# Maximum over keys and inverse of the weight sums carried to all partitions by VectorE transpositions and transfers instead of products; weights loaded once per image

## The chip, the cores and the metric

The kernel runs on one core of one Trainium2 chip. A core has five engines that run side by side, each with its own queue of instructions worked off in order: TensorE (PE, matrix products), VectorE (DVE), ScalarE (ACT), GpSimd (POOL) and SyncE (SP, which only issues transfers here). They wait for each other by semaphores. Products go from SBUF into PSUM; transfers (DMA) move data between SBUF and DRAM and are issued from the queues of SP, ACT and POOL. The metric is the device time of one execution in microseconds, as the median of several runs.

## The reference

Four images of 256 channels and 64x64 pixels go through two layers. The first is self-attention over the N = 4096 pixels with heads of 32 channels for query and key and 256 for the value:

```python
q = jnp.einsum('oc,bcn->bno', wq, xf) + bq
k = jnp.einsum('oc,bcn->bon', wk, xf) + bk[None, :, None]
attn = jax.nn.softmax(jnp.einsum('bnd,bdm->bnm', q, k), axis=-1)
v = jnp.einsum('oc,bcn->bon', wv, xf) + bv[None, :, None]
out = jnp.einsum('bcn,bmn->bcm', v, attn).reshape(B, Cc, H, W)
return gamma[0] * out + x
```

The second layer is a group norm, a clustering step (projections `f_w`, `v_w`, cosine similarity to four centres, sigmoid, one-hot of the largest, aggregation, projection back), a second group norm with an MLP of 1024 hidden channels and gelu, two batch norms with relu and a last 256x256 product. All is float32.

## The kernel before

The attention keeps keys on partitions and queries on the free axis. The 4096 queries are 8 blocks of 512 (`NB`), and for each block the 4096 keys are 8 groups of four tiles of 128. One block with one key group is a *unit*; an image has 64 units, numbered u = 8·nb + g.

- `score(u)` computes 4 products with 32 contraction rows (line 333) into two PSUM tiles. ScalarE copies them to an SBUF slot (lines 351 and 356), and VectorE keeps the running maximum over keys in `top` (lines 353 to 358): for each of the 128 partitions and each query, over all tiles so far.
- `fold(nb)` halves `top`; then `across(nb)` has TensorE transpose it in four pieces (line 369), VectorE reduce each (line 371) and lay the maxima on diagonals (`dg`, line 373); `spread` has TensorE multiply a matrix of ones with them (line 383), which puts the maximum of each query onto every partition of `mb` in PSUM. This must be done once for each block before its exponentials.
- `exps(u)`: VectorE subtracts `mb` in place (line 395), ScalarE takes the exponential (line 398), POOL adds the weights to `acc` (lines 400 and 403).
- `weigh(u, av, quarter)`: TensorE multiplies the weights with the value tile into two PSUM accumulators `av` (line 408), 8 instructions for each unit, each in two passes.
- After the block: `gather` (POOL, line 420) adds both halves of `acc`; `total` (line 429) multiplies with ones, so that the sum over all partitions stands on every partition; ScalarE copies it out (line 430), `inverse` takes the reciprocal in four pieces (line 435), `add` on POOL scales and adds the residual (lines 439 and 444).

The order is written out by hand: `weighting` runs over the 64 units and for each calls `exps(u + 1)`, the score that is due `LEAD` = 9 units ahead, the four quarters of `weigh`, and the pieces for the block before (`total` at g = 0, `inverse` at 1 and 2, `add` at 3, statistics at 5). `across` for the next block stands in unit g = 6, `spread` in g = 7. Scores live in `SLOTS` = 10 buffers of the pool `spool`, which also holds the image tiles. In images 1 to 3 the scores of the first block have been computed in the MLP of the image before; units 0 to 5 then catch up with one score every three quarters. Block 0 of each image has its maximum spread outside the loop (`alone`, or `maximum` and `first`).

After the 64 units come the cluster stage (it writes the normalised centres into the margins of `mix`, the weights for `f` and `v`, lines 115 and 703) and the MLP with `w1_s` and `w2_s`. These, and `mix`, are loaded once at the start; `derived`, called in unit 1 of image 0, turns two quarters of `w1_s` into a sum and a negative (lines 185 and 186), as the MLP uses them. SP's queue carries the loads of x (line 81) and the output (line 1115). The last block of each image already takes its sums in four products of 32 output rows (line 578).

Of the kernel before, what the change touches and what calls it, by code (L numbers as in the profile page):

```python
# [28 lines left out]
RG, GRP = 4, N // NB  # L29
LEAD, SLOTS = 9, 10  # L30

# [14 lines left out]
def attention_then_cluster_block(  # L46
# [22 lines left out]

    spool = ctx.enter_context(tc.tile_pool(name="spool", bufs=N // XT + SLOTS))  # L70
    work = ctx.enter_context(tc.tile_pool(name="work", bufs=2))
# [3 lines left out]
    ps_m = ctx.enter_context(tc.tile_pool(name="ps_m", bufs=2, space=PSUM))  # L75

    def load_x(b, t):
# [34 lines left out]

    wfv_l = spool.tile([P, KC, 2 * ED], F32, tag="s", name="wfv_l")
    nc.sync.dma_start(out=wfv_l, in_=wfv.rearrange("(k p) m -> p k m", p=P))
    mix = const.tile([P, KC, 2, 2 * ED + 32], F32, name="mix")
    for f in range(2):
        nc.gpsimd.tensor_copy(mix[:, :, f, 16 : 16 + 2 * ED], wfv_l)
    fvb = const.tile([P, 2 * ED], F32, name="fvb")
# [5 lines left out]
    nc.sync.dma_start(out=wproj_s[ED:, :], in_=pc[:, ipb : ipb + 1].rearrange("c o -> o c"))  # L124
    w1_s = loaded("w1_s", w1.rearrange("(k p) m -> p k m", p=P), [P, KC, HID])
    w2_s = loaded("w2_s", w2.rearrange("(k p) m -> p k m", p=P), [P, HID // P, C])
    wpw_s = loaded("wpw_s", wpw.rearrange("(k p) m -> p k m", p=P), [P, KC, C])
# [35 lines left out]
    ab = const.tile([P, 2], F32, name="ab")  # L163
    fb_w = const.tile([ED, P], F32, name="fb_w")
    wf_t = const.tile([ED, C], F32, name="wf_t")

    W_A, W_CD = w1_s[:, 0, : HID // 2], w1_s[:, 0, HID // 2 :]
    W_B, W_D = w1_s[:, 1, : HID // 2], w1_s[:, 1, HID // 2 :]

    def derived():  # L170
# [13 lines left out]

        nc.gpsimd.tensor_tensor(W_CD, W_CD, W_D, ALU.add)
        nc.gpsimd.tensor_scalar(W_D, W_D, -1.0, None, ALU.mult)

        nc.vector.tensor_scalar(gbv, gbv, pvc("gamma"), None, ALU.mult)
# [4 lines left out]
        for k in range(KC):  # L193
            nc.tensor.transpose(
                tps[:ED, k * P : (k + 1) * P], mix[:, k, 0, 16 : 16 + ED], ident
            )
# [49 lines left out]
    def attention(b, xs):  # L246
# [118 lines left out]
        def across(nb, tag="w2"):  # L365
# [13 lines left out]
            return dg  # L379

        def spread(nb, dg):
            mxs[nb] = ps_m.tile([P, NB], F32, tag="m", name=f"mb_{b}_{nb}")
            nc.tensor.matmul(  # L383
                mxs[nb], ones, dg.rearrange("p j n -> p (j n)"), start=True, stop=True
            )
# [40 lines left out]

        def total(nb):
            den = ps_m.tile([P, NB], F32, tag="m", name=f"den_{b}_{nb}")
            nc.tensor.matmul(den, ones, rdens[nb], start=True, stop=True)  # L429
# [33 lines left out]
        def alone():  # L463

            nc.vector.tensor_scalar(fb_w, ones[:ED], pvc("f_b", ED), None, ALU.mult)
            k_half(0)
# [44 lines left out]
        def weighting(ahead, fill, early):  # L511
            dg, av = None, None

            biased = {u: (i // KC, i % KC) for i, u in enumerate((3, 4, 5, 6, 20, 28, 36, 44))}
            for u in range(units):
# [106 lines left out]
    def cluster(b, ys, stats, cells, rest, fill, gelu):  # L622
# [9 lines left out]
        ga, gb = group_norm(b, "gn1", stats, fill, pooling)  # L632
        xns = {}

# [322 lines left out]
    def late_block(b, y, gab):  # L957
# [24 lines left out]
        def first(j, k):  # L982
            if k == 0:
# [5 lines left out]
                held["p"],  # L989
                w1_s[:, k, j * P : (j + 1) * P],  # L990
                x[:, 1, 0] if k and j >= 4 else x[:, 0, k],
# [10 lines left out]
        def second(j, c):  # L1002
            if j == 0:
                held["a", c] = ps_m.tile([P, NB], F32, tag="m", name=f"mol_{b}_{c}")
            nc.tensor.matmul(
                held["a", c],
                w2_s[:, j, c * P : (c + 1) * P],
                hidden(j),
# [42 lines left out]
    def mlp(b, ys, stats2, fill, nxt, blocks):  # L1051

        w_bcd, w_bac, w_abcd = (
# [320 lines left out]
```

## Time and profile before

| What | Time |
|---|---|
| median of 3 runs | 3479.46 us (3477.38 to 3481.62) |
| the profiled execution | 3478.09 us |
| its span | 3476.0 us |
| TensorE busy | 3421.1 us, 98% |
| VectorE busy | 2046.2 us, 59% |
| ScalarE busy | 1683.9 us, 48% |
| POOL busy | 1489.2 us, 43% |
| granted TensorE clock | 0.997 |
| `tt`, transposition (line 369), one pass | 273 ns, x128 |
| `mb`, spreading product (line 383), one pass | 592 ns (median), x64 |
| `den`, sum (line 429), one pass | 592 ns, x56 |

A product in float32 appears as two passes in the trace, each with its weight load (PEld); a transposition appears as one. Passes overlap, so the time that one takes from the queue is the distance between starts and not its duration. A row of the profile names the line, the engine, the operation, output and inputs, the shape, and how often; in a timeline the start and the time of the merged run stand in front, and the bracket at the end tells how long the engine had been idle and for whom. Lines of the waits give the total in microseconds, the number, and the longest.

### The profile page before, as it was taken

The numbers are of one execution on the slowest core, as the hardware profiler recorded it, in microseconds if no ns is written. First come the engines' busy times: TensorE is split into PE (matmuls) and PEld (weight loads), VectorE is DVE, ScalarE is ACT, GpSimd is POOL, SyncE is SP. The second block draws the span as 40 slices with busy tenths as digits, with TensorE's granted clock in tenths as the row PEclk, the third lists the DMA queues.
The fourth block names the chain that finished last, engine by engine and source line by source line (L and its number), as shares of the span: only waits on it lengthen the run. The fifth ranks groups of instructions, "written<-read, shape, count | busy, mean of one in ns | idle before, by whom it ended". The sixth has DMA issues, their size and how long they took to land.

```text
span 3476.0 us, 31760 instructions
## 1 busy us (share of the span) xinstructions
PE 3421.1 (98%) x11760; PEld 1694.3 (49%) x11760; DVE 2046.2 (59%) x2912; ACT 1683.9 (48%) x2157; POOL 1489.2 (43%) x799
## 2 busy tenths in 40 slices
PE   8999999999999999999999999999999999999999
PEld 4444445655444444565544444466554444445565
DVE  4666664645566666464556666646446666664543
ACT  5545553444554554344455555434445554544444
POOL 2656665211265665521126566552104665672200
PEclk9999999999999999999999999999999999999999
DMA  2000001000000000100000000000000000000000
GB/s 91 7 4 3 7 0 49 7 19 13 20 5 4 3 7 12 37 7 19 19 16 4 3 5 5 19 30 7 19 19 10 4 7 3 4 0 1 13 19 25
DMA packets 25260, 47.16 MB, mean 14 GB/s; under 512 B 6704, under 2 KB 8592, under 8 KB 25104
## 3 DMA queue, kind: packets, MB, share of 16 engines
q1 hardware_dynamic: 20240, 38.29, 3.2%
q10 hardware_dynamic: 4608, 6.30, 0.8%
q8 instruction: 93, 1.52, 0.2%
q0 software_dynamic: 256, 0.52, 0.1%
q14 instruction: 63, 0.52, 0.0%
HBM read 19.93 MB, written 16.78 MB: 11 GB/s over the span
## 4 chain that ended last, share of the span: by engine, by line
PE 94%; DVE 3%; ACT 1%; DMA 0%; issue 0%; SPq 0%; POOL 0%; ACTq 0%; DVEq 0%
PE av L408 52%; PE mo L1133 12%; PE sc L333 8%; PE hu L1126 4%; PE pw L1102 3%; PE hp L1126 3%; PE hq L1126 3%; PE vp L285 2%; PE fv L790 2%; PE mb L383 1%; PE den L429 1%; PE op L911 1%; PE qp L304 0%; PE kp L262 0%; PE tt L369 0%
## 5 line engine op out<-in xcount | busy, mean ns | idle before, releaser
L408 PE MATMUL av<-s,v 128*128 128x512 f32 x4096 | 1826.5, 597 | 0.6 <-ACT s L398 0.6
L408 PEld LDWEIGHTS av<-s,v 128*128 128x128 f32 x4096 | 758.9, 190 | 1024.6 <-issue 1015.1
L403 POOL TENSOR_TENSOR acc<-acc,s 128x1024 f32<-128x1024 f32 x448 | 1057.5, 2361 | 466.1 <-ACT s L398 446.7
L398 ACT ACTIVATE s<-s 128x1024 f32<-128x1024 f32 x512 | 538.7, 1057 | 462.8 <-DVE s L395 429.4
L395 DVE TENSOR_TENSOR s<-s,mb 128x1024 f32<-128x1024 f32 x512 | 595.2, 1207 | 6.5 <-PE mb L383 6.5
L1133 PE MATMUL mo<-hs,w_s 128*128 128x512 f32 x992 | 508.4, 596 | 3.8 <-ACT hs L1155 1.6
L355 DVE TENSOR_TENSOR top<-sc,top 128x1024 f32<-128x1024 f32 x196 | 239.9, 1224 | 388.0 <-PE sc L333 388.0
L1155 ACT ACTIVATE hs<-hs,pv_s 128x256 f32<-128x256 f32 x496 | 251.3, 508 | 360.9 <-DVE hs L1162 350.1
L351 ACT COPY s<-sc 128x1024 f32<-128x1024 f32 x224 | 226.1, 1009 | 350.9 <-PE sc L333 350.9
L1162 DVE TENSOR_TENSOR hs<-hu,hs 128x256 f32<-128x256 f32 x372 | 157.8, 424 | 355.0 <-ACT hs L1165 205.5
L1088 POOL TENSOR_TENSOR xn<-xn 128x256 f32<-128x256 f32 x27 | 23.8, 881 | 681.7 <-DVE xn L1075 433.4
L333 PE MATMUL sc<-q,k 32*128 32x512 f32 x2048 | 294.0, 640 | 1.4 <-DMA q<-q 1.4
L400 POOL TENSOR_TENSOR acc<-s 128x1024 f32<-128x1024 f32 x32 | 75.1, 2347 | 476.9 <-ACT s L398 476.9
L358 DVE TENSOR_TENSOR top<-sc,top 128x1024 f32<-128x1024 f32 x196 | 240.1, 1225 | 47.5 <-ACT s L351 30.9
L356 ACT COPY s<-sc 128x1024 f32<-128x1024 f32 x224 | 226.9, 1013 | 76.0 <-DVE top L355 39.8
L1162 DVE TENSOR_TENSOR hs<-hq,hs 128x256 f32<-128x256 f32 x372 | 146.4, 421 | 107.5 <-PE hq L1126 103.3
L1133 PEld LDWEIGHTS mo<-hs,w_s 128*128 128x128 f32 x992 | 186.9, 190 | 42.7 <-ACT hs L1165 7.3
L333 PEld LDWEIGHTS sc<-q,k 32*128 32x128 f32 x2048 | 81.0, 182 | 192.5 <-issue 106.6
L1126 PE MATMUL hp<-xn,w_s 128*128 128x256 f32 x496 | 150.6, 385 | 2.7 <-DVE xn L1075 2.7
L1126 PEld LDWEIGHTS hp<-xn,w_s 128*128 128x128 f32 x496 | 92.4, 190 | 73.0 <-issue 62.4
L285 PE MATMUL vp<-wv_s,x 128*128 128x256 f32 x512 | 123.4, 387 | 0.2 <-ACT v L293 0.2
L1102 PE MATMUL pw<-xn,wpw_s 128*128 128x512 f32 x248 | 112.0, 594 | 3.4 <-ACT xn L1196 2.2
(215 smaller groups left out, 2823.0 us busy)
## 6 DMA issues: line engine op xcount, KB each, us to landing
x<-in_x SPq DMA_DIRECT2D x32, 512.0 KB, 4.6
out<-xn SPq DMA_DIRECT2D x62, 256.0 KB, 2.1
q<-q ACTq DMA_DIRECT2D x96, 64.0 KB, 2.0
w_s<-in_w SPq DMA_DIRECT2D x2, 1024.0 KB, 8.9
q<-q SPq DMA_DIRECT2D x24, 64.0 KB, 2.0
q<-q POOLq DMA_DIRECT2D x8, 64.0 KB, 6.4
out<-xl SPq DMA_DIRECT2D x2, 256.0 KB, 2.0
wv_s<-in_wv SPq DMA_DIRECT2D x1, 256.0 KB, 7.1
```

Of the source, the lines that this page charges most:

```text
L333: nc.tensor.matmul(halves[r // 2][:, r % 2, :], k_s[rows, g, :], q_s[rows, :], start=True, stop=True)
L355: nc.vector.tensor_tensor(top, halves[1], top, ALU.max)
L356: nc.scalar.copy(s[:, 2:4, :], halves[1])
L358: nc.vector.tensor_tensor(top, halves[0], top, ALU.max)
L395: nc.vector.tensor_tensor(sh, sh, mxs[nb].unsqueeze(1).to_broadcast([P, 2, NB]), ALU.subtract)
L398: nc.scalar.activation(sh, sh, AF.Exp)
L403: nc.gpsimd.tensor_tensor(acc, acc, s[:, 2 * h : 2 * h + 2], ALU.add)
L408: nc.tensor.matmul(av[c], own["v"][:, RG * g + quarter, c * P : (c + 1) * P], slots[u][:, quarter, :], start=(g == 0 and quarter == 0), st ...
L1126: nc.tensor.matmul(out, w[:, j * P : (j + 1) * P], x, start=True, stop=True)
L1133: yield nc.tensor.matmul(acc[c], w2_s[:, jj, c * P : (c + 1) * P], hs[:, i], start=(j == 0 and i == 0), stop=(j == HID // P // 2 - 1 and i ...
L1155: nc.scalar.activation(dst, src, act, bias=bias)
L1162: nc.vector.tensor_tensor(dst, ps, term, ALU.add)
```

## The change

- `across`, `spread` and `inverse` are no longer used for blocks 1 to 7 of an image (block 0 keeps `across` and `spread`). In their place `highest(nb)`, in unit g = 5 behind quarter 2's score, has VectorE transpose `top` in blocks of 32x32, reduce, copy four rows of partitions beside each other, reduce and transpose again. That leaves the 512 maxima as 16 rows of 32. `everywhere` writes them to DRAM and reads them back into all 128 partitions of `mb`, both on SP's queue. `known`, in unit g = 6 before quarter 3, has ScalarE copy `mb` into PSUM, from where `exps` takes it as before.
- `total` computes the sums with four products of 32 output rows by 128 columns; one reciprocal of 128x128 follows on VectorE, and `everywhere` brings the 4 rows of 128 to all partitions of `rdens`.
- `LEAD` goes from 9 to 10. Each eleventh score lies in a new pool `swap`, in the buffer that holds `w1` in the MLP; the buffer of `w2` holds the small helper tile (`spare`), which POOL clears once per image.
- `w1`, `w2` and `mix` are loaded for each image in unit 60, and `turn_mlp` turns `w1` on POOL in unit 63. The first load of w1 and w2 and POOL's copies into `mix` at the start go; `mix` is loaded by two transfers there. `fb_w` becomes a broadcast view.

```diff
-LEAD, SLOTS = 9, 10
+LEAD, SLOTS = 10, 10
...
+    def everywhere(dst, rows, shape, name):
+
+        d = dram.tile([NB], F32, tag="row", name=f"row_{name}")
+        nc.sync.dma_start(out=d.rearrange("(a b) -> a b", a=shape), in_=rows)
+        nc.sync.dma_start(out=dst, in_=d.partition_broadcast(P))
...
+    def load_mix(b):
+        own_w["mix"] = swap.tile([P, KC, 2, 2 * ED + 32], F32, tag="mix", name=f"mix_{b}")
+        for f in range(2):
+            nc.sync.dma_start(
+                out=own_w["mix"][:, :, f, 16 : 16 + 2 * ED],
+                in_=wfv.rearrange("(k p) m -> p k m", p=P),
+            )
...
+    def load_mlp(b):
+
+        w1_s = own_w["w1"] = swap.tile([P, KC, HID], F32, tag="w1", name=f"w1_{b}")
+        w2_s = own_w["w2"] = swap.tile([P, HID // P, C], F32, tag="w2", name=f"w2_{b}")
+        nc.sync.dma_start(out=w1_s, in_=w1.rearrange("(k p) m -> p k m", p=P))
+        nc.sync.dma_start(out=w2_s, in_=w2.rearrange("(k p) m -> p k m", p=P))
...
+    def turn_mlp():
+
+        _, w_cd, _, w_d = own_w["q"]
+        nc.gpsimd.tensor_tensor(w_cd, w_cd, w_d, ALU.add)
+        nc.gpsimd.tensor_scalar(w_d, w_d, -1.0, None, ALU.mult)
...
-            s = slots[u] = spool.tile([P, RG, NB], F32, tag="s", name=f"s_{b}_{u}")
+            pool, tag = (swap, "w1") if u % (SLOTS + 1) == SLOTS else (spool, "s")
+            s = slots[u] = pool.tile([P, RG, NB], F32, tag=tag, name=f"s_{b}_{u}")
...
+        def spare():
+            if "w2" not in own:
+                own["w2"] = swap.tile([P, 3, P], F32, tag="w2", name=f"few_{b}")
+                nc.gpsimd.memset(own["w2"], 0.0)
+            return own["w2"]
+
+        def highest(nb):
+
+            top = tops.pop(nb)
+            fl = top[:, 1]
+            nc.vector.transpose(fl, top[:, 0])
+            low = spare()[:, nb % 2]
+            mx = low[:, :16]
+            nc.vector.tensor_reduce(mx, fl.rearrange("p (c n) -> p c n", n=D), AX.X, ALU.max)
+            four = low[:D, D : D + 64].rearrange("p (r c) -> p r c", r=4)
+            for r in range(4):
+                nc.vector.tensor_copy(four[:, r], mx[r * D : (r + 1) * D])
+            one = low[:D, 3 * D : 4 * D]
+            nc.vector.tensor_reduce(
+                one[:, :16], low[:D, D : D + 64].rearrange("p (r c) -> p c r", r=4), AX.X, ALU.max
+            )
+            nc.vector.transpose(low[:D, :D], one)
+            mb = work.tile([P, NB], F32, tag="w2", bufs=1, name=f"mr_{b}_{nb}")
+            everywhere(mb, low[:16, :D], 16, f"mx_{b}_{nb}")
+            return mb
+
+        def known(nb, mb):
+            mxs[nb] = ps_m.tile([P, NB], F32, tag="m", name=f"mb_{b}_{nb}")
+            nc.scalar.copy(mxs[nb], mb)
...
             den = ps_m.tile([P, NB], F32, tag="m", name=f"den_{b}_{nb}")
-            nc.tensor.matmul(den, ones, rdens[nb], start=True, stop=True)
-            nc.scalar.copy(rdens[nb], den)
-
-        def inverse(nb, pieces):
-            for i in pieces:
-                r = rdens[nb][:, i * P : (i + 1) * P]
-                nc.vector.reciprocal(r, r)
+            for j in range(4):
+                nc.tensor.matmul(
+                    den[j * D : (j + 1) * D, :P],
+                    ones[:, :D],
+                    rdens[nb][:, j * P : (j + 1) * P],
+                    start=True,
+                    stop=True,
+                )
+            rec = spare()[:, 2]
+            nc.vector.reciprocal(rec, den[:, :P])
+            everywhere(rdens[nb], rec[::D], 4, f"rd_{b}_{nb}")
...
-            at.update({divmod(3 * i + 2, RG): GRP + i for i in range(7)})
+            at.update({divmod(3 * i + 2, RG): GRP + i for i in range(8)})
+        else:
+            at[0, 2], at[0, 0] = at[0, 0], GRP + 1
...
+                if u == units - 4:
+                    load_mix(b)
+                    load_mlp(b)
+                elif u == units - 1:
+                    turn_mlp()
...
                 if g == GRP - 1 and more:
-                    spread(nb + 1, dg)
                     exps(u + 1)
...
-                    elif g < 3:
-                        inverse(nb - 1, (2 * g - 2, 2 * g - 1))
...
                 if g == GRP - 2 and more:
-                    dg = across(nb + 1)
+                    known(nb + 1, mb)
                 due(u, 3)
+                if g == GRP - 3 and more:
+                    mb = highest(nb + 1)
```

More of the change, by code (lines that the diff above doesn't have):

```diff
@@ L70, in attention_then_cluster_block @@
     spool = ctx.enter_context(tc.tile_pool(name="spool", bufs=N // XT + SLOTS))
+    swap = ctx.enter_context(tc.tile_pool(name="swap", bufs=1))
     work = ctx.enter_context(tc.tile_pool(name="work", bufs=2))
@@ L75, in attention_then_cluster_block @@
     ps_m = ctx.enter_context(tc.tile_pool(name="ps_m", bufs=2, space=PSUM))
+    dram = ctx.enter_context(tc.tile_pool(name="dram", bufs=2, space=bass.MemoryType.DRAM))
+    def everywhere(dst, rows, shape, name):
+        d = dram.tile([NB], F32, tag="row", name=f"row_{name}")
+        nc.sync.dma_start(out=d.rearrange("(a b) -> a b", a=shape), in_=rows)
+        nc.sync.dma_start(out=dst, in_=d.partition_broadcast(P))
     def load_x(b, t):
@@ L111, in attention_then_cluster_block @@
     )
[L113 to L117, printed above, removed]
+    own_w = {}
+    def load_mix(b):
[5 more added lines that the diff above has]
+            )
+    load_mix("first")
     fvb = const.tile([P, 2 * ED], F32, name="fvb")
@@ L124, in attention_then_cluster_block @@
     nc.sync.dma_start(out=wproj_s[ED:, :], in_=pc[:, ipb : ipb + 1].rearrange("c o -> o c"))
-    w1_s = loaded("w1_s", w1.rearrange("(k p) m -> p k m", p=P), [P, KC, HID])
-    w2_s = loaded("w2_s", w2.rearrange("(k p) m -> p k m", p=P), [P, HID // P, C])
     wpw_s = loaded("wpw_s", wpw.rearrange("(k p) m -> p k m", p=P), [P, KC, C])
@@ L163, in attention_then_cluster_block @@
     ab = const.tile([P, 2], F32, name="ab")
-    fb_w = const.tile([ED, P], F32, name="fb_w")
     wf_t = const.tile([ED, C], F32, name="wf_t")
-    W_A, W_CD = w1_s[:, 0, : HID // 2], w1_s[:, 0, HID // 2 :]
-    W_B, W_D = w1_s[:, 1, : HID // 2], w1_s[:, 1, HID // 2 :]
+    fb_w = pv_s[:ED, PV["f_b"] : PV["f_b"] + 1].to_broadcast([ED, P])
+    def load_mlp(b):
[3 more added lines that the diff above has]
+        nc.sync.dma_start(out=w2_s, in_=w2.rearrange("(k p) m -> p k m", p=P))
+        own_w["q"] = [
+            w1_s[:, k, h * HID // 2 : (h + 1) * HID // 2] for k in range(KC) for h in range(2)
+        ]
+    def turn_mlp():
+        _, w_cd, _, w_d = own_w["q"]
+        nc.gpsimd.tensor_tensor(w_cd, w_cd, w_d, ALU.add)
+        nc.gpsimd.tensor_scalar(w_d, w_d, -1.0, None, ALU.mult)
     def derived():
@@ L183, in derived @@
         nc.vector.tensor_tensor(dw_e, dw_e, lsb1, ALU.add)
-        nc.gpsimd.tensor_tensor(W_CD, W_CD, W_D, ALU.add)
-        nc.gpsimd.tensor_scalar(W_D, W_D, -1.0, None, ALU.mult)
         nc.vector.tensor_scalar(gbv, gbv, pvc("gamma"), None, ALU.mult)
@@ L194, in derived @@
             nc.tensor.transpose(
-                tps[:ED, k * P : (k + 1) * P], mix[:, k, 0, 16 : 16 + ED], ident
+                tps[:ED, k * P : (k + 1) * P], own_w["mix"][:, k, 0, 16 : 16 + ED], ident
             )
@@ L463, in alone @@
         def alone():
-            nc.vector.tensor_scalar(fb_w, ones[:ED], pvc("f_b", ED), None, ALU.mult)
             k_half(0)
@@ L511, in weighting @@
         def weighting(ahead, fill, early):
-            dg, av = None, None
+            mb, av = None, None
             biased = {u: (i // KC, i % KC) for i, u in enumerate((3, 4, 5, 6, 20, 28, 36, 44))}
@@ L632, in cluster @@
         ga, gb = group_norm(b, "gn1", stats, fill, pooling)
-        xns = {}
+        xns, mix = {}, own_w["mix"]
         def norm(nb):
@@ L989, in first @@
                 held["p"],
-                w1_s[:, k, j * P : (j + 1) * P],
+                own_w["w1"][:, k, j * P : (j + 1) * P],
                 x[:, 1, 0] if k and j >= 4 else x[:, 0, k],
@@ L1006, in second @@
                 held["a", c],
-                w2_s[:, j, c * P : (c + 1) * P],
+                own_w["w2"][:, j, c * P : (c + 1) * P],
                 hidden(j),
@@ L1051, in mlp @@
     def mlp(b, ys, stats2, fill, nxt, blocks):
+        W_A, W_CD, W_B, W_D = own_w["q"]
+        w2_s = own_w["w2"]
         w_bcd, w_bac, w_abcd = (
```

## The prediction

> **What bounds the kernel now.** I read the page's busy times and chain first, then the waits of the tensor engine, then its timeline over three units of the weighting stage. A unit is four key tiles of 128 keys against one block of 512 queries.
>
> ```profile
> PE 3421.1 (98%) x11760; PEld 1694.3 (49%) x11760; DVE 2046.2 (59%) x2912; ACT 1683.9 (48%) x2157; POOL 1489.2 (43%) x799
> PE 94%; DVE 3%; ACT 1%; DMA 0%; issue 0%; SPq 0%; POOL 0%; ACTq 0%; DVEq 0%
> ```
>
> TensorE (PE) is busy for 98% of the span and 94% of the chain that ended last runs through it. Busy can hide slow matmuls, so the next question is whether it waits.
>
> ```profile
> PE cnt L841 <- DVE scr L760: 9.9, 4, 2.7
> PE kp L262 <- DMA x<-in_x: 9.6, 3, 8.7
> ...
> PE sc L333 <- DMA q<-q: 1.4, 1, 1.4
> ...
> PE av L408 <- ACT s L398: 0.6, 1, 0.6
> ```
>
> Columns: microseconds in total, times, longest. The long waits belong to the cluster stage and the first load. In the weighting stage, where this change lies, 4096 passes of `av` wait 0.6 us together. There an instruction taken off TensorE's queue shortens the run by its own time, until another engine comes late.
>
> What the removed products cost is read from the distance between neighbouring scores:
>
> ```profile
> 1159.52 1.14 PE L333 MATMUL sc<-q,k 32*128 32x512 f32 x8
> 1160.59 7.13 PE L408 MATMUL av<-s,v 128*128 128x512 f32 x16
> 1167.65 1.14 PE L333 MATMUL sc<-q,k 32*128 32x512 f32 x8
> ...
> 1175.79 1.14 PE L333 MATMUL sc<-q,k 32*128 32x512 f32 x8
> ...
> 1182.12 0.60 PE L369 MATMUL tt<-ident,top 128*128 128x128 f32 x4
> ...
> 1184.36 1.14 PE L333 MATMUL sc<-q,k 32*128 32x512 f32 x8
> 1185.43 1.12 PE L383 MATMUL mb<-dg,ones 128*128 128x512 f32 x2
> ...
> 1193.36 1.14 PE L333 MATMUL sc<-q,k 32*128 32x512 f32 x8
> ...
> 1197.96 1.02 PE L429 MATMUL den<-rden,ones 128*128 128x512 f32 x2
> ...
> 1202.35 1.14 PE L333 MATMUL sc<-q,k 32*128 32x512 f32 x8
> ```
>
> A plain unit takes 1167.65 - 1159.52 = 8.13 us. The unit with the four transpositions takes 8.57 (0.44 more), the one with the spreading product 9.00 (0.87 more), the one with the sum 8.99 (0.86 more). Durations of single matmuls (273 and 592 ns) overlap and would mislead.
>
> **The change part by part.**
>
> *Removed from TensorE.* Transpositions and spreading product go in 7 blocks of each of 4 images, 28 times (block 0 keeps them): 28 x (0.44 + 0.87) = 36.7 us. The Trainium skill (TensorE: Matmul & The Clock Gate, Part 4: PE-mode transpose) gives about 275 ns for one transposition in a kernel's context. That would make four of them 1.10 us and the removal 28 x 0.66 = 18.5 us larger. The distances say 0.44 for four, so I keep the trace.
>
> *The sum of the weights.* One product of 512 columns becomes four of 32 output rows by 128 columns. The last block of each image already does just that, in eight passes:
>
> ```profile
> 590.56 0.42 PE L578 MATMUL den<-rden,ones 128*32 128x128 f32 x8
> 590.92 1.99 PE L285 MATMUL vp<-wv_s,x 128*128 128x256 f32 x8
> ```
>
> The next product starts 0.36 us after the first of them. The bounds are 0.21 (a quarter of 0.86, perfect overlap) and 0.86 (none); I take 0.36. Saved: 28 x (0.86 - 0.36) = 14.0 us. TensorE gains 36.7 + 14.0 = 50.7 us.
>
> *Added on VectorE for the maximum.* Per block: a 128x512 transposition, a 128x512 reduction, four copies, a small reduction and a 32x32 transposition. No row shows a VectorE transposition. The nearest is the reduction of as many elements (L371, 692 ns). Lower bound: nothing; upper bound: 2.5 us, four operations of L371's size, if its 32-wide blocks were handled apart. I take 0.69. The small ones follow the rows of 0.15 to 0.19 us that small VectorE instructions show near 80 us. Sum: 0.69 + 0.69 + 4 x 0.16 + 0.2 + 0.2 = 2.4 us, with gaps about 2.7. Off VectorE go L371 and L373 (1.38) and three of four reciprocals (L435, 3 x 0.92 = 2.8), so its total falls.
>
> *The transfers.* Each vector goes to DRAM and is read back by all partitions: two dependent transfers on SP's queue, 56 pairs in all.
>
> ```profile
> out<-xn SPq DMA_DIRECT2D x62, 256.0 KB, 2.1
> ...
> q<-q SPq DMA_DIRECT2D x24, 64.0 KB, 2.0
> ```
>
> I take 2.0 for the small write, 2.5 for the 256 KB read (bounds 2.0 and the 4.6 of the 512 KB loads of x) and 0.6 us of issue before each (L319's median on SP's queue is 588 ns): 5.7 us for the pair. [...] The row of `out` is a write to HBM and landed in 2.1. [...]
>
> What hides the 5.7? Let the score that completes the maximum start at 0, in unit 5 of a block. By the rows after 1167.65, VectorE ends its second maximum at 3.8. Fold 0.7, statistics (L448) 1.3 and the new 2.7 us end near 8.4. Behind them is queued the subtraction for unit 7 (2.3), to 10.7, against the need at 16.3. Transfers land at 14.1. The copy into PSUM (`known`, 0.6 us as L430 was) stands in ScalarE's queue after unit 6's score copies, which end near 15. Behind it wait the copies of the next score and then the exponentials of the next block, which TensorE needs at 25.5. From the end of `known` these need about 4.5 us (copy 1.0, maximum 1.2, subtraction 1.2, exponential 1.1), so it may end at 21. The pair may take about 12 us. Cost taken: nothing; beyond 12, one for one. The inverse has three units (24 us) before `add` on POOL asks for it. SP's queue holds x's loads only from unit 56 on; in front of the last inverse stands one x tile of two transfers whose slot is free.
>
> *Where LEAD 10 costs.* In image 0, score 10 moves directly behind score 9, with the same two PSUM buffers:
>
> ```profile
> 66.58 1.65 PE L333 MATMUL sc<-q,k 32*128 32x512 f32 x8
> ...
> 70.28 1.23 DVE L358 TENSOR_TENSOR top<-sc,top 128x1024 f32<-128x1024 f32 x1 [0.79 <-ACT s L351]
> 71.42 2.34 DVE L395 TENSOR_TENSOR s<-s,mb 128x1024 f32<-128x1024 f32 x2
> 71.79 1.14 PE L333 MATMUL sc<-q,k 32*128 32x512 f32 x8
> ```
>
> The buffers come free at 71.5; score 9 ends near 67.7, and the weighting that filled this time now stands behind. Carried on to unit 2, I get 3.2 us lost.
> In images 1 to 3, score 15 comes before quarter 3 of unit 5, one quarter (1.7 us) ahead of score 16, and its evacuation takes 2.6: 0.9 us lost. VectorE then does fold and maximum before the subtraction for unit 7. I also charge a wait for the new POOL clearing of the helper tile, behind POOL's additions (L403, 4.8 us). That moves the exponentials, and ScalarE's copies of score 16 behind them, so that the second half of score 17 waits about 1.1. Together 3 x 2 = 6 us (bounds 0 and 12).
>
> *Weights per image.* Two 1 MB loads (8.9 us each) and `mix` are issued in unit 60, behind x, in slots free by then; the first use is behind unit 63, three units of 7 us later. POOL's sign changes (1.27 + 1.50) fall in unit 63, after `gather` and before the cluster stage asks POOL. Nothing, or 2.8 us per image if that cover is missing. At the start 2 MB fewer stand in the DMA engines beside the first `q` transfers: up to the 1.4 us of the wait above; I take 1.4.
>
> Sum against the profiled span of 3476.0: -50.7 + 3.2 + 6 - 1.4 = -42.9, a span of 3433. That execution took 3478.1 us, 1.4 under the median of the runs (3479.5), so I subtract from the median: 3437.
>
> **The rivals.**
> *Smaller gain.* New waits eat part: scores 15 to 17 collide harder, or VectorE's transposition is dear and delays the subtractions. For: VectorE has 3.3 us free in a plain unit (8.13 - 4.8) and the new work is 2.7 in one piece. Against: it is at one unit in eight, and VectorE's waits for scores total 388 us. At the upper bounds of all terms, and 0.3 us per block: 3437 + 6 + 1.4 + 8.4 = 3453.
> *Slower.* The pair of transfers is late, ScalarE stops in `known`, scores and exponentials stop behind it. It costs 28 us per microsecond beyond 12; the forecast's gain of 43 is gone at 13.5 us. At 15 us: 3437 + 84 = 3521. For: while the start loads the queues, landings of 6.4 (q on POOL's queue) and 10.7 us (wpw) are seen. Against: in the weighting stage the DMA share is near 0 and landings are 2.0.
> *No change.* The products lay in time that TensorE had free anyway. The distances of 0.44, 0.87 and 0.86 speak against it. 3479.
>
> **How the numbers follow.** Forecast 0.62, smaller gain (3445 to 3472) 0.28, larger gain (below 3425) 0.04, no change 0.02, slower 0.04. The range of 3425 to 3455 has the full overlap of the sum product and no new waits at its lower end (28 x 1.96 = 54.9 saved) and the rival of smaller gain at its upper. A measurement of this kernel tells 0.2% (7 us) from no change. So faster 0.94, same 0.02, slower 0.04.
>
> **What would show it.** The distance between scores around the maximum falls to 8.1 in all but the unit of the sum (8.5); `av` still waits for almost nothing; `known`'s copy is not preceded by idle time on ScalarE that ends with the transfer, or does so without a wait on TensorE; one gap of 3 to 4 us near 68, and one or two of about 1 us in the sixth to eighth unit of images 1 to 3. The prediction is wrong if transfers land after more than 6 us each, or if TensorE's waits for `s` or for score buffers grow beyond some 20 us.

## The result and the profile after

The changed kernel takes 3447.36 us (median of 4 runs, 3442.2 to 3451.53), beside 3478.63 us for the kernel before in the same rounds (4 runs, 3477.38 to 3481.62). The ratio is 0.9908, with a 95% interval of 0.9891 to 0.9925: 0.9% faster. The forecast was 3437, the range 3425 to 3455. The profiled execution of the changed kernel took 3450.09 us, with a span of 3448.3; the span is 27.7 us shorter than before, where the prediction's sum has 42.9.

TensorE is still what bounds the kernel. From the page of the changed kernel, busy times and the chain that ended last:

```profile
PE 3390.0 (98%) x11760; PEld 1673.2 (49%) x11760; DVE 2002.3 (58%) x2995; ACT 1678.9 (49%) x2157; POOL 1489.6 (43%) x807
...
PE 94%; DVE 4%; ACT 1%; issue 1%; DMA 0%; SPq 0%; ACTq 0%; DVEq 0%
```

PE's busy time fell by 31.1 us, VectorE's by 43.9. Its waits (microseconds in total, times, longest):

```profile
PE sc L359 <- ACT s L382: 6.8, 7, 3.0
...
PE av L464 <- ACT s L454: 0.6, 1, 0.6
```

The first line is new: scores wait 6.8 us for ScalarE to free their buffers, in seven places. TensorE waits for no transfer of the maximum or of the inverse. ScalarE does wait, before the copy `known` of block 7 in each image, but no wait of TensorE follows:

```profile
ACT mb L435 <- DMA mr<-row_mx: 8.2, 4, 2.7
```

What the products gave is read as before, from the distance between neighbouring scores in TensorE's timeline:

```profile
182.62 1.14 PE L359 MATMUL sc<-q,k 32*128 32x512 f32 x8
...
190.76 1.14 PE L359 MATMUL sc<-q,k 32*128 32x512 f32 x8
...
198.89 1.14 PE L359 MATMUL sc<-q,k 32*128 32x512 f32 x8
199.96 3.70 PE L464 MATMUL av<-s,v 128*128 128x512 f32 x8
203.59 0.43 PE L488 MATMUL den<-rden,ones 128*32 128x128 f32 x8
203.95 3.70 PE L464 MATMUL av<-s,v 128*128 128x512 f32 x8
207.58 1.14 PE L359 MATMUL sc<-q,k 32*128 32x512 f32 x8
```

Units with the maximum now take 8.13 and 8.14 us, as plain ones do. The unit with the sum takes 8.69. The three together take 207.58 - 182.62 = 24.96, against 1202.35 - 1175.79 = 26.56 before: 1.60 us per block.

The new path of the maximum, in the timelines of VectorE, SP's queue and ScalarE (image 1):

```profile
968.12 0.71 DVE L417 STREAM_TRANSPOSE top<-top 128x512 f32<-128x512 f32 x1
968.93 0.69 DVE L420 TENSOR_REDUCE few<-top 128x16 f32<-128x512 f32 x1
969.66 0.69 DVE L423 COPY few<-few 32x16 f32<-32x16 f32 x4
...
970.93 0.33 SPq L84 DMA_DIRECT2D row_mx<-few  x1
972.29 0.34 SPq L85 DMA_DIRECT2D mr<-row_mx  x1
...
977.28 0.60 ACT L435 COPY mb<-mr 128x512 f32<-128x512 f32 x1
```

The whole of it on VectorE takes 2.7 us. The last line has no bracket: the copy `known` starts when ScalarE comes to it, and not when the read lands. So it is in 24 of the 28 blocks; the other four are the blocks 7 above. The transfers' sizes and median landings:

```profile
row_mx<-few SPq DMA_DIRECT2D x28, 2.0 KB, 1.3
mr<-row_mx SPq DMA_DIRECT2D x28, 256.0 KB, 3.1
```

So the pair lands 1.3 + 3.1 = 4.4 us after its first issue, or a little later. The prediction took 2.0 for the small write and 2.5 for the read: the one is faster, the other slower.

Where the 27.7 us came from, adding up the two profiled executions (the weighting stage of an image is taken from its first `av` to its last `den`):

| part | predicted, us | measured, us |
|---|---|---|
| products, 28 blocks | 50.7 | 45.1 (1.61 each) |
| start, first `av` at 60.91 instead of 62.95 | 1.4 | 2.0 |
| image 0, first unit | -3.2 | -4.9 |
| images 1 to 3 | -6 | -4.4, -2.7, -4.4 = -11.5 |
| everything else | 0 | -3.0 |
| sum | 42.9 | 27.7 |

The loss in the first unit of image 0, in TensorE's timeline of the changed kernel:

```profile
64.54 1.65 PE L359 MATMUL sc<-q,k 32*128 32x512 f32 x8
...
69.17 1.47 PE L359 MATMUL sc<-q,k 32*128 32x512 f32 x8 [2.99 <-ACT s L382]
70.57 5.40 PE L464 MATMUL av<-s,v 128*128 128x512 f32 x8
```

The wait of 2.99 us ahead of score 10 is the gap that the prediction named. Behind it stands what it did not name: eight passes of `av` take 5.40 us, where a gap-free run of eight takes 3.70 (in an experiment below). The same in images 1 and 2, where the scores stand alike:

```profile
967.13 1.41 PE L359 MATMUL sc<-q,k 32*128 32x512 f32 x8 [0.50 <-ACT s L382]
...
975.54 1.13 PE L359 MATMUL sc<-q,k 32*128 32x512 f32 x4
977.44 1.13 PE L359 MATMUL sc<-q,k 32*128 32x512 f32 x4 [0.78 <-ACT s L382]
978.50 8.83 PE L464 MATMUL av<-s,v 128*128 128x512 f32 x16
...
1832.85 1.13 PE L359 MATMUL sc<-q,k 32*128 32x512 f32 x4 [0.78 <-ACT s L382]
1833.91 7.13 PE L464 MATMUL av<-s,v 128*128 128x512 f32 x16
```

Score 17 is cut in two by a wait of 0.78 us. Since each half takes 1.13 us, as long as a whole score, 2.96 us pass until the next `av` (975.54 to 978.50) instead of 1.07: 1.9 lost. Score 16 waits 0.50 and runs 0.27 longer. Together this is the 2.7 us that image 2 loses. The waits are equal in image 1, but sixteen passes take 8.83 us there and 7.13 in image 2. The granted clock tells why. Six stretches of the changed kernel, each with its length, then busy time of PE, PEld, VectorE, ScalarE and POOL (with their instructions), the granted TensorE clock, the DMA share and GB/s:

```profile
67.36:70.77 3.41, 1.60 (x9) 0.80 (x10) 1.40 (x3) 2.18 (x3) 3.33 (x2) 1.00 0.00 0
70.77:74.18 3.41, 3.41 (x5) 1.35 (x5) 2.90 (x3) 1.60 (x2) 0.33 (x1) 0.50 0.01 2
975.31:978.72 3.41, 2.63 (x10) 0.82 (x10) 1.14 (x2) 2.34 (x3) 3.25 (x3) 1.00 0.00 0
978.72:982.13 3.41, 3.41 (x5) 1.35 (x5) 3.31 (x3) 2.15 (x3) 0.62 (x1) 0.50 0.00 0
1832.05:1835.46 3.41, 2.63 (x10) 1.14 (x9) 1.33 (x2) 3.39 (x5) 2.61 (x2) 1.00 0.01 2
1835.46:1838.87 3.41, 3.41 (x10) 1.50 (x9) 3.37 (x3) 1.89 (x3) 0.00 (x0) 1.00 0.00 0
```

In images 0 and 1 a stretch of exactly 3.41 us runs at clock 0.50, behind one in which TensorE was little used; it costs 1.7 us where TensorE is busy throughout. Image 2 is spared. Image 3 loses the same 4.4 us as image 1. Over the whole span, half-clock time is 20.5 us before the change, in 4 places, and 41.0 us after it, in 9 places (leaving out the one in which the execution ends); that is 10 us more at most, if TensorE were busy in all of it. Of the 15.2 us that are missing, the clock took 8.1: 1.7 in image 0, 3.4 in images 1 and 3, and the 3.0 of "everything else", where TensorE's work is what it was. These 3.0 stand where the steps of half clock were added: behind image 0's weighting stage there is one step more, and 1.5 us more until the next stage; behind image 3's there are two more, and 1.4 us; behind images 1 and 2, with as many steps as before, the difference is below 0.1 us. The products took 5.6, and the waits of images 1 to 3 another 2.1; the start gave 0.6 back.

### The profile page after: what moved, and what is told of

It is laid out like the page before. It is cut to its first block, busy times and chain, and to the rows that moved or that the text cites. A ratio compares the mean times of both kernels' runs of the same rounds, so it can differ in the third digit from the quotient of the medians.

```text
span 3448.3 us, 32176 instructions
## 1 busy us (share of the span) xinstructions
PE 3390.0 (98%) x11760; PEld 1673.2 (49%) x11760; DVE 2002.3 (58%) x2995; ACT 1678.9 (49%) x2157; POOL 1489.6 (43%) x807
## 4 chain that ended last, share of the span: by engine, by line
PE 94%; DVE 4%; ACT 1%; issue 1%; DMA 0%; SPq 0%; ACTq 0%; DVEq 0%
PE av L464 52%; PE mo L1202 12%; PE sc L359 8%; PE hu L1195 4%; PE pw L1171 3%; PE hp L1195 3%; PE hq L1195 3%; PE vp L310 2%; PE fv L857 2%; PE op L978 1%; PE qp L329 0%; PE kp L287 0%; PE agg L887 0%; DVE vf L866 0%; DVE hs L1231 0%
## 5 line engine op out<-in xcount | busy, mean ns | idle before, releaser
L1202 PE MATMUL mo<-hs,w 128*128 128x512 f32 x992 | 507.7, 595 | 3.8 <-ACT hs L1224 1.6
L1157 POOL TENSOR_TENSOR xn<-xn 128x256 f32<-128x256 f32 x27 | 23.9, 887 | 682.0 <-DVE xn L1144 459.8
L1202 PEld LDWEIGHTS mo<-hs,w 128*128 128x128 f32 x992 | 186.6, 190 | 42.5 <-ACT hs L1234 7.8
L1195 PE MATMUL hp<-xn,w 128*128 128x256 f32 x496 | 150.6, 385 | 2.6 <-ACT v L318 2.6
L1195 PEld LDWEIGHTS hp<-xn,w 128*128 128x128 f32 x496 | 92.4, 190 | 72.9 <-issue 62.4
```

Of the source, the lines that this page charges most:

```text
L1195: nc.tensor.matmul(out, w[:, j * P : (j + 1) * P], x, start=True, stop=True)
L1202: yield nc.tensor.matmul(acc[c], w2_s[:, jj, c * P : (c + 1) * P], hs[:, i], start=(j == 0 and i == 0), stop=(j == HID // P // 2 - 1 and i ...
```

## The experiments

The theories, as the expectations name them. A: the gain of the products is real, and what is missing went where LEAD 10 puts its scores (the waits and the halved clock behind them) and into a sum product that is dearer than taken. B: the transfers reach their users late. C: what is missing is the clock in stages that the change does not touch, so that no placement brings it back. The edits are against the changed kernel unless another is named. A ratio is to the kernel before, and stands where a kernel was timed in rounds; without one, the time is that of one run, and since the changed kernel's own runs lie 9.3 us apart, such a run is read by its stages and waits rather than by its total.

### The extra score of image 0 put elsewhere

```diff
-            at[0, 2], at[0, 0] = at[0, 0], GRP + 1
+            for i in range(6):
+                del at[i, 0]
+            at[0, 0] = GRP + 1
+            at.update({divmod(3 * i + 2, RG): GRP + 1 + i for i in range(1, 7)})
```

> The changed kernel with the scores of image 0 alone spread (scores 9 to 15 three quarters apart). Theory A: no wait near 67 us and no lowered clock there; the weighting stage of image 0 falls from 521.2 to 516.3; images 1 to 3 stay at 519 to 521.

Measured: 3439.6 us, span 3437.8, 10.5 us below the changed kernel's. Image 0's stage takes 517.17 us instead of 521.21, and the wait of 2.99 us is gone (a later score, at 85.17, now waits 0.45). The other 6 us came in places that were not edited: images 1 to 3 took 519.3 us each, with the same waits as before but with no halved clock behind them, and half-clock time fell to 23.9 us. So the place of score 10 costs what A says, and where the clock halves later on depends on what happened earlier.

### The gap filled instead of removed

```diff
                 due(u, 0)
+                if u == 0 and not b:
+                    junk = ps_m.tile([P, NB], F32, tag="m", name="junk")
+                    for _ in range(3):
+                        nc.tensor.matmul(junk, ones, slots[0][:, 0, :], start=True, stop=True)
```

Three products are added whose result nobody reads; they run while score 10 waits.

> The changed kernel with three products of 512 columns whose result nobody reads, between scores 9 and 10 of image 0, where TensorE waits 3.0 us. Theory A (the wait also halves TensorE's clock): no clock below 1 in the window from 60 to 80 us, the eight passes of weighting behind score 10 take 3.7 us instead of 5.4, and the weighting stage of image 0 falls from 521.2 to 519.5. Rival (the slow passes are due to contention of the two scores' evacuation): they stay at 5.4.

Measured: 3444.53 us, span 3442.7. TensorE's timeline of this kernel:

```profile
66.32 2.84 PE L603 MATMUL junk<-s,ones 128*128 128x512 f32 x6
69.38 1.47 PE L359 MATMUL sc<-q,k 32*128 32x512 f32 x8 [0.22 <-ACT s L382]
70.78 3.70 PE L464 MATMUL av<-s,v 128*128 128x512 f32 x8
```

and the two stretches of its clock record that answer to the first two above:

```profile
68.03:71.44 3.41, 3.19 (x13) 1.21 (x12) 1.76 (x2) 2.18 (x3) 3.21 (x2) 1.00 0.00 0
71.44:74.86 3.42, 3.42 (x12) 1.33 (x14) 2.91 (x3) 1.14 (x2) 0.00 (x0) 1.00 0.01 2
```

Score 10 still starts no earlier (69.38 against 69.17), because its buffers come free when they did. But the clock stays at 1.00, and the eight passes behind it take 3.70 instead of 5.40. Image 0's stage is 519.52 us, the expected 519.5: 1.7 us of its loss was the clock alone, and the useless work brought it back.

### The extra scores of all images spread

The edit above for image 0, and for images 1 to 3:

```diff
-            at.update({divmod(3 * i + 2, RG): GRP + i for i in range(8)})
+            at.update({divmod(3 * i, RG): GRP + i for i in range(8)})
```

> The changed kernel with its two collisions of scores undone: in image 0 scores 9 to 15 come three quarters apart, in images 1 to 3 scores 8 to 15 start at quarter 0 instead of quarter 2, so that score 15 is three quarters ahead of score 16. Theory A (the missing gain is waits of TensorE for score buffers, and its clock halved for 3.4 us after some of them): the waits of TensorE for ScalarE at the score line, 6.8 us, go to below 1; the weighting stages take 521.2, 521.0, 519.3 and 521.0 us and fall to about 516.6 each; median 16 us lower, near 3431. Theory B (the gain is lost where vectors arrive late by transfer, in ScalarE's copy): no change, 3447. Theory C (the gain is lost to halved clock in the other stages, whatever the waits): 11 us lower at most, clock still near 0.994.

Measured: 3437.48 us, ratio 0.9882 (0.9866 to 0.9899). This is 10 of the 16 us that A expected, with no transfer touched. (Between the profiled executions it is 13.3 us: the changed kernel's lay 2.7 us above its median, and the expectation was taken from its losses.) The waits of TensorE for score buffers:

```profile
PE sc L359 <- ACT xn L1184: 1.4, 3, 0.5
...
PE sc L359 <- ACT s L382: 0.5, 1, 0.5
```

6.8 us became 0.5, but the new pattern begins with a score ahead of the first `av` of images 1 to 3, and there it waits 0.5 us three times for a buffer that the stage before still holds (first line). The stages take 517.18 and three times 515.40 us; the latter leave out a score of 1.1 us that now stands ahead of them. That is within 1 us of the 516.3 that 527.6 less seven blocks of 1.61 would leave. What is still missing lies outside the weighting stages, where the half-clock time is 23.9 us.

### The sum beside a score

```diff
                 due(u, 0)
+                if nb and g == 0:
+                    total(nb - 1)
...
                 if nb:
-                    if g == 0:
-                        total(nb - 1)
-                    elif g == 3:
+                    if g == 3:
```

> The changed kernel with the small products of the sum directly behind the score of unit 0 of a block. Theory A: the distance of scores in that unit falls from 8.69 to 8.49 us (the change of array use is paid once), 5.6 us in all. Rival: no change of that distance.

Measured: 3440.1 us, span 3438.0. TensorE's timeline around the sum:

```profile
200.43 1.14 PE L359 MATMUL sc<-q,k 32*128 32x512 f32 x8
201.50 0.42 PE L488 MATMUL den<-rden,ones 128*32 128x128 f32 x8
201.85 7.13 PE L464 MATMUL av<-s,v 128*128 128x512 f32 x16
208.92 1.14 PE L359 MATMUL sc<-q,k 32*128 32x512 f32 x8
```

The unit takes 8.49 us instead of 8.69, with the same instructions in another order. The four products of 32 output rows cost 0.36 us from start to start, as predicted, in both places. What differs is the `av` around them. In the changed kernel's rows above, the eight passes on each side of the sum take 3.63 us (199.96 to 203.59, and 203.95 to 207.58), 7.26 in all; here the sixteen take 7.07 in one run (201.85 to 208.92). In the trace, passes start 0.43 us apart, but the last of a run takes 0.52 until a product on part of the array starts, and the first behind one takes 0.53: each end of a run costs 0.1, and splitting the run costs 0.2. That such a change costs time agrees with a statement of the Trainium skill (TensorEngine Tiling (Array Packing), Key Properties), that changing the tiling mode drains TensorE; it gives no time, and the 0.1 for each change is from these rows. From the score to the small products no such cost shows (200.43 to 201.50, 1.07 us, as from a score to `av` at 198.89), although they use the array in different ways (32 rows by 128 columns, then 128 by 32). The gain of 5.6 us that this term lacked (28 x 0.2) is thus recovered; the rest of the 10.3 us that the span fell by is the clock (half-clock time 30.7 us).

### One part alone: the sum

The kernel before with the new `total` and its transfers, without `inverse`; nothing else of the change but `fb_w` as a broadcast view, which the kernels of the next two sections have, too.

```diff
             den = ps_m.tile([P, NB], F32, tag="m", name=f"den_{b}_{nb}")
-            nc.tensor.matmul(den, ones, rdens[nb], start=True, stop=True)
-            nc.scalar.copy(rdens[nb], den)
+            for j in range(4):
+                nc.tensor.matmul(
+                    den[j * D : (j + 1) * D, :P], ones[:, :D],
+                    rdens[nb][:, j * P : (j + 1) * P], start=True, stop=True,
+                )
+            rec = rdens[nb][:, :P]
+            nc.vector.reciprocal(rec, den[:, :P])
+            everywhere(rdens[nb], rec[::D], 4, f"rd_{b}_{nb}")
```

> The kernel before with the new sum and inverse alone (four small products, one reciprocal, the transfers); the maximum by products as before, LEAD 9, weights loaded once. Theory A: the four small products cost 0.56 us of TensorE's queue and not 0.36, so 28 x (0.86 - 0.56) = 8.4 us less, 3470. By the prediction's 0.36 it would be 14.0 less, 3465.

Measured: 3469.42 us (7 runs), ratio 0.997 (0.9959 to 0.9982), 10.5 us below the kernel before. From 197.07 to 205.76 its sum unit takes 8.69 us, instead of 8.99: 0.3 us per block and 8.4 in all come from TensorE, most of what was gained.

### One part alone: the maximum

The kernel before with `highest`, `known` and `everywhere` in the places where `across` and `spread` were called (units 6 and 7 of a block, one unit later than in the changed kernel); LEAD stays 9, the weights stay loaded.

```diff
                 if g == GRP - 1 and more:
-                    spread(nb + 1, dg)
+                    known(nb + 1, mb)
                     exps(u + 1)
...
                 if g == GRP - 2 and more:
-                    dg = across(nb + 1)
+                    mb = highest(nb + 1)
```

> The kernel before with the new path for the maximum alone; sum and inverse as before, LEAD 9, weights loaded once. Theory A: 28 x (0.44 + 0.87) = 36.7 us less, 3442. Theory B (transfers come late): the distance between scores in unit 7 and the next stays above 8.13 us and less than half is gained, above 3460.

Measured: 3455.87 us, ratio 0.9936 (0.9921 to 0.9951), some 14 us above what was expected. In blocks 1 to 6 all units but those of the sum take 8.1 us, so the products gave what they should. The loss lies in block 7 of each image. From the timeline there (image 0), queues and engines:

```profile
518.93 0.33 SPq L82 DMA_DIRECT2D mr<-row_mx  x1
519.37 6.84 SPq L89 DMA_DIRECT2D x<-in_x  x4
...
523.44 0.59 ACT L413 COPY mb<-mr 128x512 f32<-128x512 f32 x1 [9.67 <-DMA mr<-row_mx]
...
528.13 2.08 PE L442 MATMUL av<-s,v 128*128 128x512 f32 x2 [2.80 <-ACT t L458]
```

Four loads of x are issued right behind `mr`, which then lands 523.44 - 518.93 = 4.5 us after its issue, instead of the usual 3.1. Unit 55 and those behind it have no score ahead and take about 6.9 us instead of 8.1, so TensorE arrives early. ScalarE waits in `known` for the transfer; behind it stand the exponentials, and behind these the copy `t` that empties the buffer for `av`. Image 3, which has no further x to load, is the control: there `mr` lands 3.0 us after its issue, and TensorE still waits 1.30 us. So about half of the other waits (2.80, 2.25 and 2.90) is the later place of `highest`, and the rest the loads beside it. TensorE's waits for that copy (total, times, longest):

```profile
PE av L442 <- ACT t L458: 9.2, 4, 2.9
```

In three of the four images the clock halves behind this wait, which is 1.7 us each. 9.2 + 5.1 = 14.3, beside the 14.5 us by which the four stages (522.96, 522.67, 523.31 and 520.05 us) miss 28 x 1.31 = 36.7. So B holds in this one place, block 7, if `highest` comes a unit later. The changed kernel has it a unit earlier and does not pay this.

### Both paths without LEAD 10 and without reloading weights

The kernel of the maximum alone with the sum's new `total` added. `few`, a tile of 128x128 cleared once, takes the place of the helper tile that the changed kernel puts into the buffer of `w2`.

> The kernel before with both new paths (maximum and inverse by transposition and transfer, sum in four small products) and nothing else of the change: LEAD stays 9, all scores in the old slots, the weights loaded once, the helper tile a small constant; the maximum is taken in unit 6 after quarter 2 and copied to PSUM in unit 7. Theory A: the products alone bring 28 x (0.44 + 0.87 + 0.30) = 45 us and no new waits come, since the pair of transfers takes 4.5 us and has some 7: 3434. Theory B: the shorter lead makes ScalarE wait in the copy and TensorE behind it; at 1 us per block 3462, slower than the changed kernel.

Measured: 3439.81 us, ratio 0.989 (0.9876 to 0.9905). The same kernel with the sum beside the score, as above:

> As the run with LEAD 9, and the four small products of the sum stand directly behind the score of unit 0 of a block instead of between quarters 1 and 2. Theory A: a change between a product that uses the whole array and one that uses part of it costs 0.1 us on each side; beside the score this is paid once, the distance of scores in that unit falls from 8.69 to 8.49 us, and 28 x 0.2 = 5.6 us are gained against the run with LEAD 9: 3428. Rival: the 0.56 us are the products' own time, no change.

Measured: 3430.26 us, ratio 0.9862 (0.9847 to 0.9876). The wait in block 7, in the first kernel's list of waits:

```profile
PE av L442 <- ACT t L458: 5.8, 4, 1.6
```

In the second's the same line has 4.5 us in four waits, the longest of 1.3. The stages take 517.9 to 518.1 us in the first and 516.2 to 516.5 in the second, where the clock halved in none of them. So the gain needs neither the eleventh score nor the weights loaded per image. What LEAD 10 allows, `highest` a unit earlier and so no wait in block 7 (4.5 to 5.8 us), is worth less than what its scores cost where the change puts them (waits of 6.8 us, and the clock behind them).

### The transfers made late

To find where the transfers' slack ends, the vector of the maximum is sent through DRAM n more times before it is read back.

```diff
         nc.sync.dma_start(out=d.rearrange("(a b) -> a b", a=shape), in_=rows)
+        if name[0] == "m":
+            for i in range(3):
+                e = dram.tile([NB], F32, tag=f"hop{i}", name=f"hop{i}_{name}")
+                nc.sync.dma_start(out=e.rearrange("(a b) -> a b", a=shape), in_=d.rearrange("(a b) -> a b", a=shape))
+                d = e
```

> The changed kernel with three more copies from DRAM to DRAM in the path of the maximum, which at 1.4 us each or somewhat more arrive 4 to 6 us later than the 4.5 us after the transposition. Theory A (the path has about 12 us): TensorE's waits for ScalarE at the score line grow by less than 3 us in all and the time stays within 5 us of the changed kernel. Theory B (transfers already cost time): every microsecond is paid, 28 x 4 = 112 us or more.

Measured: 3470.71 us, span 3468.9, 20.6 us above the changed kernel's. The copy `known` in block 7 of image 0, and what followed:

```profile
525.83 0.59 ACT L440 COPY mb<-mr 128x512 f32<-128x512 f32 x1 [8.54 <-DMA mr<-hop_mx]
...
530.53 1.86 PE L469 MATMUL av<-s,v 128*128 128x512 f32 x3 [2.91 <-ACT t L485]
```

In block 2 of image 0 the data come 10.1 us after the transposition's end at 183.71. ScalarE waits 3.60 us for them (`known` starts at 193.84), and TensorE does not wait at all. In block 7 they come after 11.9 us (x's loads are issued beside them), and TensorE waits 2.91 us. So the slack there is about 9 us. TensorE's waits for `t` are 18.3 us in all: 9.7 in block 7 of the four images, and the rest in seven of the other 24 blocks. Three of these are among blocks 2 to 6, where the data came after 10.66, 12.12 and 12.17 us and TensorE waited 0.17, 1.62 and 1.68: a slack of 10.5 us each time. The other four are blocks 1; in images 1 and 3 the slack of that block is 8.0 us. Half-clock time rose from 41.0 to 44.3 us, which costs up to 1.7; the sum of 20.0 accounts for the loss. The expectation missed because the slack is 12 us in no block.

With eight more trips:

> The same with eight more copies: 11 to 16 us later, 16 to 20 in all. Theory A with a slack of 12 us: TensorE waits 4 to 8 us in each of 28 blocks, 110 to 230 us more. If the slack is larger than I read, less; if it is none, 310 us or more.

Measured: 3782.66 us, span 3780.9. SP's queue, ScalarE and TensorE in block 2:

```profile
196.20 0.32 SPq L84 DMA_DIRECT2D row_mx<-few  x1
...
215.37 0.59 ACT L440 COPY mb<-mr 128x512 f32<-128x512 f32 x1 [12.67 <-DMA mr<-hop_mx]
...
217.87 2.42 PE L364 MATMUL sc<-q,k 32*128 32x512 f32 x8 [5.50 <-ACT s L387]
...
221.41 0.67 ACT L485 ACTIVATE t<-av,pv_s 128x512 f32<-128x512 f32 x1
...
222.14 5.41 PE L469 MATMUL av<-s,v 128*128 128x512 f32 x8 [1.85 <-ACT t L485]
```

The data come 19.2 us after the first issue (215.37 - 196.20), and TensorE waits 5.50 + 1.85 = 7.35 us for what stands behind them. The score between the two waits ran at half clock, 2.42 us instead of 1.14, which hides 1.28 us of the second. TensorE is thus 8.6 us late, and 19.2 - 8.6 = 10.6 us would have cost nothing in this block, about the 10.5 of the kernel above and not the prediction's 12. The difference is the copy `t`. It stands behind the exponentials in ScalarE's queue, and `av` needs its buffer, too: from the end of `known` (215.96) to the end of `t` (222.08) it takes 6.1 us, where the prediction counted 4.5 to the exponentials. With a small delay `t` is what comes late first; all of TensorE's new waits with three more trips are for it. The kernel lost 333 us, 12 per block, more than was expected. Scores and `av` wait 245.8 us in all, 239 more than in the changed kernel. The other 94 us fit the clock, which was halved for 361.8 us, part of them while TensorE waited: a late block costs its wait and then a slower TensorE.

### Spread scores and the sum beside a score

The edit of all images with `3 * i + 1` in place of `3 * i`, which keeps the first extra score behind the stage's first products, and the sum moved as above.

> The changed kernel with scores 9 to 15 of image 0 three quarters apart, scores 8 to 15 of images 1 to 3 begun at quarter 1 (so that score 15 is two quarters, 3.4 us, ahead of score 16, which is more than its evacuation of 2.6), and the small products of the sum directly behind the score. Theory A: the 0.5 us waits for score 8 at the start of an image, which the start at quarter 0 had, are gone; against the run with all scores spread (3437.5) 5.6 us less from the sum and 2 to 4 us from those waits and the clock behind them: about 3429. If the clock is halved as often as in the changed kernel all the same, 3439.

Measured: 3429.81 us, ratio 0.9856 (0.984 to 0.9872). Stages of 515.72, 516.72, 516.73 and 517.00 us; one wait of a score per image remains, 2.2 us in all (0.48 in images 1 and 2, 0.77 in image 3). This and the kernel without LEAD 10 with the sum beside the score are the two that are faster than both kernels, with intervals wholly below the changed kernel's, and they can't be told apart from each other. The second is much the simpler.

## Why the prediction was right, and where it was off

The direction, the bound and the mechanism were right; two terms of the sum were too small, and one was absent. The measured gain is 31.3 us where 42.9 were forecast. All misses but one (the start) went the same way, and 3447 lies in the forecast's range and in the band of the rival "smaller gain" (3445 to 3472) at once. That the range held it is in part luck: its upper end made room for new waits of 0.3 us in every block, and what filled that room was the sum's price and the clock. It was not "the upper bounds of all terms" either, since the sum's own bound of 0.86 (14.0 us) is not in it.

- *TensorE bounds, and what leaves its queue shortens the run.* Right: the units of the maximum fell to 8.13 us, the full 0.44 and 0.87. The distances were the right view. The 275 ns of the Trainium skill (TensorE: Matmul & The Clock Gate, Part 4: PE-mode transpose) would have made the gain 18.5 us larger, and the units' distances show no such excess: as the duration of one transposition 275 agrees with the trace's 273 ns, but four took 0.44 us from the queue.
- *The sum: "I take 0.36".* Off: 0.56, in bounds of 0.21 to 0.86. The distance that was read holds the small products alone; the change from and to whole-array products is paid in the passes before and behind them. Moving the products beside a score brought the price to 0.36. The gain was taken 28 x 0.2 = 5.6 us too large.
- *VectorE: 2.4, with gaps 2.7 us.* Right: 2.7, and the transposition of 128x512 took 0.71 beside the 0.69 taken. (The upper bound of 2.5 should read 2.8, four times 0.69; nothing rests on it.)
- *The pair of transfers, 5.7 us, hidden by a slack of 12.* The cost of nothing was right. The pair takes 4.4 us and a little, and `known` starts 4.5 to 6.4 us after the transposition. The slack is 10.5 us in the blocks 2 to 6, 1.5 less than derived, because the chain behind `known` left out the copy `t`. It is 8.0 in block 1 of images 1 and 3, and about 9 in block 7; neither was looked at apart. The units of block 7 have no scores, and loads of x are issued there. The rival "slower" was wrong in size: behind a wait the clock falls, so that a late block costs more than its wait.
- *LEAD 10 in image 0: 3.2 us.* The gap was in its place, 2.99 us long. The loss was 4.9, by 1.7 us of half clock behind it.
- *LEAD 10 in images 1 to 3: 2 us each.* 2.7 us without the clock (image 2), 4.4 with it (images 1 and 3). The waits are where they were foretold and shorter, 0.50 (0.9 foretold) and 0.78 (1.1). What the step left out is that a score cut in two runs twice as long: 1.9 us for a wait of 0.78.
- *Start: 1.4.* 2.0 measured; the wait for the first `q` is gone. The kernels that load the weights once, with the new paths or without, start their first `av` at 62.6 to 62.9 us, those that load them per image at 60.6 to 61.5.
- *Weights per image: nothing.* No wait for them shows in the changed kernel.
- *The clock, absent from the sum.* About 8 us: 1.7 + 3.4 + 3.0. This is the largest single miss. The four runs of the changed kernel follow it: 3442.2, 3444.64, 3450.09 and 3451.53 us at mean clocks of 0.996, 0.995, 0.994 and 0.993.

B holds in block 7 alone, with `highest` a unit later. C holds in part: some 3 us, and the scatter from run to run. A explains the rest, and the two best kernels gain 47.7 and 49.3 us against the kernel before, near the 50.7 that the products were to give.

## What to carry to other kernels

Where one engine sets the end, cost an edit by the distances between its neighbouring instructions, and read the distance with the same neighbours that the instruction will have: a product on a part of the array was 0.2 us dearer between whole-array products than beside another part-array product. Count a new wait on TensorE together with the clock that may halve behind it, which cost 1.7 us here even behind a wait of 0.78. A slack that is read in one period of a loop holds for that period: look apart at the first and the last one, where other work starts or stops and the next loads begin. And count in it everything that stands in the waiting engine's queue behind the late instruction: here a copy behind the exponentials took 1.5 us of it.

## What the hardware showed unasked

- *When the clock halves.* In the clock records of the kernel before, the changed kernel and nine of these experiments (all but the late transfers), each half-clock period begins on one grid of 3.413 us that runs through the execution, and lasts one or two of its steps. Between the first weighting and the end, the step ahead of a period had TensorE idle for 1.4 us or more in all cases but two, and no step with more than 2 us idle was followed by full clock; between 1.4 and 1.9 us both occur. Taken 0.30 us earlier (a shift chosen to fit; 0.25 to 0.31 do), the steps of full clock part cleanly, at half of their length, 1.71 us: those with up to 1.69 us idle kept the full clock, and those with 1.71 or more lost it, 58 of the 60 periods. The Trainium skill (TensorE: Matmul & The Clock Gate, Part 1) has the same free-running step of 3413 ns; it asks for an idle step, or a gap of more than about 3.4 us, before the clock falls. Here half a step was enough, as the wait of 2.99 us, of which 1.81 fell into one step, shows beside the filled gap.
- *Two periods that do not fit.* They are in images 1 and 3 of the changed kernel: in image 1 the step ahead (975.31 to 978.72 above) has 0.78 us of idle time, and `av` for 0.52 us only, the rest being scores; in image 2 the grid falls otherwise, the step has the same 0.78 us, but `av` for 1.55, and the clock stays. So it may be that scores count for less than whole-array products. But with scores spread in image 0 alone, the same wait in image 1 fell into a step (971.25 to 974.66, taken 0.30 us earlier) with 0.78 us idle and 2.25 of scores, and the clock stayed; the step ahead of image 3's period in the changed kernel (2661.19 to 2664.60) has the same two figures. What decides in such steps is open.
- *Why unchanged stages moved.* As the grid does not move with the program, every edit shifts all later waits against it (read from one trace of each kernel). Stages without an edited instruction so changed by a few microseconds: the 3.0 us of "everything else" in the table, and images 1 to 3 in the first experiment.
- *A broadcast read slows beside loads.* 256 KB read from a row of 2 KB land after 3.1 us, but after 4.5 us with four loads of x issued behind them; in the same kernel's image 3, without such loads, after 3.0.
